# A tuned two-layer image kernel: softmax bookkeeping moved between engines, the last tile of a Winograd-type convolution summed in another order, and one tiny product moved

## The chip, the cores and the metric

The kernel runs on one core of one Trainium2 chip. The metric is the device time of that core in microseconds (us), the median of three runs. All data are 32-bit floats (f32). In what follows TensorE is PE, VectorE is DVE, ScalarE is ACT, GpSimd is POOL and SyncE, which only issues transfers here, is SP.

## The reference, cut to what matters

The input is `x` of shape (4, 256, 48, 48): four images, 256 channels, 2304 pixels each. Layer 0 is what the change touches:

```
h   = relu(batchnorm(conv3x3(groupnorm(x))))            # 256 -> 256 channels
q,k,v = qkv_w @ h + bias, 8 heads of 32 channels
attn = softmax(q^T k / sqrt(32))                          # 2304 x 2304 per head
x   = x + proj_w @ (v attn^T) + bias
```

Layer 1 normalizes the result, makes 45 softmax weights per pixel, applies five dilated 3x3 branches with them, mixes the six parts with a 1x1 convolution, normalizes over the batch and adds its input. It is not touched, but for images 1 to 3 its products share PE with the next image's convolution.

## The kernel before, in words

Per image b the kernel runs the 3x3 convolution, then q, k and v (`conv_qkv`), then the attention (`attention`), then layer 1 (`dynamic_filters`). The convolution and q, k, v of images 1 to 3 are fed into the layer 1 of the image before: a planner (`Clock`, `either`, `busy_dve`, the `need` and `free` entries) holds estimated times for each engine while the program is built, and by these it sets the order of PE's instructions and which engine does an elementwise step. The order is fixed when the program is built; on the chip every engine runs its own list in order, and semaphores tie the lists together.

**Attention.** An image's work is nine *units*. Units 0 to 7 are four heads (one half of the channels) by 512 queries; unit 8 is the last 256 queries of both halves. A unit has 18 steps, one for each 128 keys. A step m of unit u has these parts:

- `scores`: four products for four heads, one into the one-bank PSUM tile `so` (one buffer), three into the three-bank tile `se` (two buffers, shared with the denominators `den` and the projection `pp`).
- two exponentials on ACT, `p[:,0]` from `so` (L1350) and `p[:,1:]` from `se` (L1351).
- `weigh`: the numerator products of the step before, summed over the 18 steps in the PSUM tile `num` (one buffer, so the next unit's first product waits until `num` has been copied to `ao`), and the running sum `acc` of the exponentials on DVE (L1390). Five steps of a unit, the entries of `LENT` (two in unit 0, four in unit 8), *lend* three heads of their sum to a transfer from POOL's queue that adds `p[:,1:]` into a part of the tile `ring` called `extra` (L1392, L1394).

At the end of a unit ACT copies `num` (L1400) and DVE adds `extra` to `acc` (L1397). `close(u)` runs at step 1 of unit u+2: PE sums `acc` over the keys into `den` (L1406), and DVE transposes, inverts, transposes and multiplies (L1418 to L1428). `close(7)` runs at step 2 of unit 8. In unit 8 a product with a zero tile first clears the four heads' `num` (L1372), because its two halves write different columns. The order of the program in a step is: scores of this step, a `close` if due, `weigh` of the step before.

**Convolution of images 1 to 3** (`conv_blocks`). Along rows and along columns it uses sums of inputs and outputs, so that a tile (i, o) is four products n = 0 to 3 in two rotating PSUM buffers (`psc`). Product 0 is copied as `one`; products 0 and 1 give `two` (sum and difference); products 2 and 3 are joined with `two` to `y`; `after` adds the row term (`d12`, made in `before`) and asks for the relu (L1126) that writes `hid`. The last tile of the twelve is (5, 1), and the first q product (L1256) needs its relu.

**q, k, v.** Nine pairs of v products take turns in the same two PSUM buffers and are copied by ACT (L1285). `pb` (L1294) is a product of two columns that gives the bound of the scores, copied by DVE (L1295); it stands behind the last v.

**`ring`** also holds the convolution's weights: `taken(t)` has SP load 1024 columns for tile t; tile 0's are columns 2048 to 3071, loaded ahead of the attention.

Of the kernel before, what the change touches and what calls it, by code (L numbers as in the profile page):

```python
# [17 lines left out]
P = 128  # L18
# [40 lines left out]
def conv_preact_kernel(  # L59
# [493 lines left out]
    with tc.tile_pool(name="w", bufs=1) as wpool, tc.tile_pool(  # L553
# [554 lines left out]
        def conv_blocks(b, psum_tile, blocks, pool, hid):  # L1108
# [23 lines left out]
            def before(i, o):  # L1132

                s12, d12, s34, d34 = (blocks.held[:, j, o] for j in range(4))
                if i == 0:
                    t = spare.pop(0)
                    axpy(t, s34, -4.0, s12)
                    relu(o, 2, t, clock.both(800))
                    either(s12, s12, s34, ALU.subtract)
                elif i == 5:  # L1140
                    t = spare.pop(0)
                    axpy(t, d34, -2.0, d12)
                    relu(o, 1, t, clock.both(800))
                    axpy(d12, d34, -8.0, d12)
                    clock.both(800)

            def target(i, o):

# [3 lines left out]
                    return blocks.held[:, 1 if i == 2 else 3, o]  # L1152
                return spare.pop(0)

            def after(i, o, y):

                s12, d12, s34, d34 = (blocks.held[:, j, o] for j in range(4))
                if i in (2, 4):
                    s, d = (s12, d12) if i == 2 else (s34, d34)
                    either(s, y, blocks.first[o], ALU.add)  # L1160
                    either(d, blocks.first[o], y, ALU.subtract)
                elif i in (0, 5):
                    relu(o, i and 3, y, either(y, y, s12 if i == 0 else d12, ALU.add))

            blocks.scaled()
            need[0] = lambda: 150 + max(slot("c", 2), blocks.end[STEPS[0]])
            for t, (i, o) in enumerate(TILES):
                u = us.pop(t)
                y = target(i, o).rearrange("p (n s) -> p n s", s=2)
                for n, j in enumerate((1, 2, 0, 3)):  # L1170
                    m = psum_tile(f"pc_{b}_{i}_{o}_{j}")[:, :XN]
                    clock("PE", 0, slot("c", 2), blocks.end[i, j])
                    z = blocks.of[i].rearrange("p (j h n) -> p j h n", j=4, h=NH)[:, j]
                    relus(max(clock.t["ACT"], clock.t["PE"]))
                    for h in range(NH):
                        nc.tensor.matmul(
                            m, u[:, h, j], z[:, h], start=(h == 0), stop=(h == NH - 1)
                        )
                        clock("PE", MM * XN / CH)
                        if h == 0:  # L1180
                            need[0] = lambda: 0.0
                            if t == 1 and n == 3:
                                blocks.along(ORDER[1])
                            if n == 0:
                                if t + 2 < len(TILES):
                                    us[t + 2] = taken(t + 2)
                                before(i, o)
                            yield MM * XN / CH
                    if n == 0:
                        one = pool.tile([P, XN], F32, tag="one", name=f"one_{b}_{i}_{o}")  # L1190
                        nc.scalar.copy(one, m)
                        end = clock("ACT", 400, clock.t["PE"])
                    elif n == 1:
                        two = pool.tile([P, 2, XN], F32, tag="two", name=f"two_{b}_{i}_{o}")
                        if busy_dve():
                            nc.scalar.copy(two[:, 1], m)
                            end = clock("ACT", 400, clock.t["PE"])
                            either(two[:, 0], one, two[:, 1], ALU.add, end)
                            either(two[:, 1], one, two[:, 1], ALU.subtract, end)
                        else:  # L1200
                            tt(two[:, 0], m, one, ALU.add)
                            tt(two[:, 1], one, m, ALU.subtract)
                            end = clock("DVE", 900, clock.t["PE"], end)
                    else:
                        to = y[:, :, n - 2]
                        if busy_dve():
                            nc.scalar.mul(to, m, 1.0 if j == 0 else -1.0)
                            end = clock("ACT", 450, clock.t["PE"])
                            either(to, to, two[:, n - 2], ALU.add, end)
                        else:  # L1210
                            if j == 0:
                                tt(to, m, two[:, 0], ALU.add)
                            else:
                                tt(to, two[:, 1], m, ALU.subtract)
                            end = clock("DVE", 480, clock.t["PE"])
                        if n == 3:
                            after(i, o, y.rearrange("p n s -> p (n s)"))
                    free["c"].append(end)
                    then = STEPS[4 * t + n + 1] if 4 * t + n + 1 < len(STEPS) else None
                    need[0] = lambda: 150 + max(  # L1220
                        slot("c", 2), blocks.end.get(then, NEVER) if then else last[0],
                    )
                    if n == 3 and o == NH - 1:
                        blocks.passed.add(i)
                    if then is None:
                        relus(NEVER)
                        last[0] = clock.t["ACT"]
                    yield MM * XN / CH
# [4 lines left out]
        def conv_qkv(b, gn, psum_tile, weights, ready, pool, between=()):  # L1233
# [40 lines left out]
            for t in range(0, NT, 2):  # L1274
# [15 lines left out]
                    nc.vector.tensor_tensor(top[:, 0], top[:, 0], top[:, 1], ALU.mult)  # L1290
                    nc.vector.tensor_scalar(top[:, 0], top[:, 0], QS, None, ALU.mult)
                yield 4 * MM * C / CH
            pb = psum_tile(f"pb_{b}")
            nc.tensor.matmul(pb[:, :NH], hmat, top[:, 0], start=True, stop=True)  # L1294
            nc.vector.tensor_copy(bound[:, b, :], pb[:, :NH])  # L1295

        qkv = {}
        CONV_QKV = MM * (6 * 4 * 6 * TN / CH + NCK * NH * 4 + NT * 2 * C / CH)
# [6 lines left out]
        def attention(b, q, k_, vT, pools, spare, project, scratch, following):  # L1305
# [1 line left out]

            ps_s, ps_a, work0 = pools
            ao = keep("h", f"ao_{b}")
            zeros = work0.tile([P, D], F32, tag="zeros", name=f"zeros_{b}", bufs=1)  # L1310
            nc.gpsimd.memset(zeros, 0.0)

            extra = scratch.rearrange("p (j n) -> p j n", j=3)
            scratch = work0.tile([P, QC], F32, tag="rt", name=f"rt_{b}", bufs=1)

            whole, rest = N // QC * QC, N % QC
# [39 lines left out]
            def weigh(u, m, p):  # L1356
# [3 lines left out]
                        acc=work0.tile([P, 4, QC], F32, tag="acc", name=f"acc_{b}_{u}"),  # L1360
                    )
                st = state[u]
                several, end = len(units[u]) > 1, u == last
                if end and m >= NT - 2:
                    sums(u, p, m == NT - 2, m == NT - 1)
                    if m == NT - 2:
                        sums(u, st["acc"], False, False)
                        sums(u, extra, False, False, 1)
                if several and m == 0:

                    for j, r in enumerate(heads):
                        nc.tensor.matmul(st["num"][r, :], zeros, p[:, j, :], start=True, stop=False)  # L1372
                for i, (g, q0, n, at) in enumerate(units[u]):
                    for j, r in enumerate(heads):
                        nc.tensor.matmul(  # L1375
                            st["num"][r, at : at + n],
                            vT[:, m, g * P + j * D : g * P + (j + 1) * D],
                            p[:, j, at : at + n],
                            start=(m == 0 and not several),
                            stop=(m == NT - 1 and i == len(units[u]) - 1),  # L1380
                        )
                if end and m >= NT - 2:
                    return
                if m == 0:
                    st["first"] = p
                else:
# [2 lines left out]
                    js = slice(0, 1 if lend else 4)  # L1389
                    nc.vector.tensor_tensor(st["acc"][:, js], other[:, js], p[:, js], ALU.add)  # L1390
                    if lend and m == lends(u)[0]:
                        nc.gpsimd.dma_start(out=extra, in_=p[:, 1:])  # L1392
                    elif lend:
                        nc.gpsimd.dma_start(out=extra, in_=p[:, 1:], accum_op=ALU.add)  # L1394
                if m == NT - 1 and not end:
                    rest = st["acc"][:, 1:]
                    nc.vector.tensor_tensor(rest, rest, extra, ALU.add)  # L1397
                if m == NT - 1 and not end:
                    g, q0, n, _ = units[u][0]
                    nc.scalar.copy(ao[:, g, q0 : q0 + n], st["num"])  # L1400

            def sums(u, rhs, start, stop, first=0):
                if start:
                    state[u]["den"] = three(f"den_{b}_{u}")[:, 0, :]
                for j, r in enumerate(heads[first:]):
                    nc.tensor.matmul(  # L1406
                        state[u]["den"][r, :], ones, rhs[:, j, :], start=start, stop=stop
                    )

            def close(u):  # L1410

                if u < last:
                    sums(u, state[u]["acc"], True, True)
                else:
                    busy(ps_a.tile([P, 512], F32, tag="one", name="warm"), 5)
                st = state.pop(u)
# [15 lines left out]
            for i, (u, m) in enumerate(steps):  # L1432
# [5 lines left out]
                if prev is not None:  # L1438
                    weigh(*steps[i - 1], prev)
                prev = ps  # L1440
                if m == 2 and u == last:
                    close(u - 1)
                if m == 6 and (u % NH == 1 or u == last):
                    while (chunk + 1) * CH <= units[u if u == last else u - 1][0][1]:
# [935 lines left out]
        for b in range(B + 1):  # L2380
# [176 lines left out]
            if b == B - 1:  # L2557
# [1 line left out]
                    out=pads[B % 2].rearrange("p h r w -> p (h r w)")[:, : NH * (2 + NF) * CH],  # L2559
                    in_=late_d[0].rearrange("p m c -> p (m c)"),  # L2560
                )
            scratch = ring[:, : 3 * QC]
            spare = []
            following = [lambda: None] * 2
            clear(pads[b % 2] if b else pads[1])
            if b + 1 < B:
                load_pad(b + 1)
                us[0] = taken(0)

                def opened(b=b):  # L2570
                    coming.append(Blocks(b + 1, pads[(b + 1) % 2]))
                    coming[-1].stage0()
                    us[1] = taken(1)
# [97 lines left out]
```

## Time and profile before

| what | us |
|---|---|
| median of three runs | 2675.72 |
| lowest and highest of them | 2675.06, 2680.87 |
| the profiled execution, its own time | 2675.02 |
| its span, first to last instruction | 2673.2 |
| PE busy | 2586.6 (97%) |
| DVE busy | 2080.8 (78%) |
| ACT busy | 1802.6 (67%) |
| POOL busy | 789.6 (30%) |

Busy times are counted from the records of the instructions, and a matmul's end is modelled, so that a busy PE may be one that waits; only starts are to be relied on. A row of the timeline has the start, the length, the engine (PEld are PE's weight loads), the line, the operation, the output and inputs, the shape and the count; in square brackets the idle time of the engine before it and what ended that. The four attentions begin at 151, 798, 1446 and 2069 us.

### The profile page before, as it was taken

To read this page: it belongs to the slowest core of one execution; us is meant where nothing else is said; L and a number is where in the kernel's file an instruction comes from. 1 tells how busy PE (TensorE), PEld (TensorE's weight loads), DVE (VectorE), ACT (ScalarE), POOL (GpSimd) and SP (SyncE) were. 2 spreads that over 40 slices of the span, in tenths; PEclk is the share of its full clock that TensorE was granted. 3 is DMA by queue.
4 is the path that set the end of the run, shared out by engine and by line. 5 is a ranking of instruction groups with operands and counts; after the bars stand their busy time and mean duration, and the time that the engine had idled before them with its cause. 6 is when DMAs were issued, how large, how long until landed. Compare 5 with 4: busy or idle time off the path is not lost. (4 is left out here: it accounts for less than half of the span.)

```text
span 2673.2 us, 42578 instructions
## 1 busy us (share of the span) xinstructions
PE 2586.6 (97%) x16952; PEld 1092.1 (41%) x16952; DVE 2080.8 (78%) x2045; ACT 1802.6 (67%) x2281; POOL 789.6 (30%) x885
## 2 busy tenths in 40 slices
PE   7999999999999999999999999999989999999996
PEld 5632222555562222355555222245546222235554
DVE  7768998858739898967764989895775889895676
ACT  4479898734449999854445998984444989884344
POOL 4201001286520011057750001007765000100453
PEclk9999999999999999999999999999999999999998
DMA  4815445323252445433324354452324544433456
GB/s 174 225 42 107 101 101 114 92 65 103 70 108 72 101 95 114 102 81 89 95 63 91 89 113 101 101 108 79 89 69 125 128 106 95 107 84 79 121 165 222
DMA packets 138094, 279.96 MB, mean 105 GB/s; under 512 B 58152, under 2 KB 98512, under 8 KB 136864
## 3 DMA queue, kind: packets, MB, share of 16 engines
q0 software_dynamic: 27408, 144.00, 23.1%
q1 hardware_dynamic: 110480, 133.17, 18.9%
q8 instruction: 135, 2.21, 0.3%
q14 instruction: 71, 0.58, 0.1%
HBM read 112.12 MB, written 36.04 MB: 55 GB/s over the span
## 5 line engine op out<-in xcount | busy, mean ns | idle before, releaser
L1390 DVE TENSOR_TENSOR acc<-acc,p 128x2048 f32<-128x2048 f32 (+1 forms) x568 | 1039.3, 1830 | 96.7 <-ACT p L1351 46.2
L1351 ACT ACTIVATE p<-se 128x1536 f32<-128x1536 f32 x648 | 938.7, 1449 | 0.0
L1340 PE MATMUL se<-q,k 32*128 32x512 f32 (+1 forms) x4320 | 737.0, 593 | 0.0
L1340 PE MATMUL so<-q,k 32*128 32x512 f32 (+1 forms) x1440 | 728.3, 593 | 3.5 <-DVE bound L1295 2.0
L1375 PE MATMUL num<-p,vT 128*32 128x512 f32 (+1 forms) x5760 | 699.4, 561 | 1.7 <-ACT ao L1400 1.7
L1350 ACT ACTIVATE p<-so 128x512 f32<-128x512 f32 x648 | 388.5, 600 | 158.7 <-PE se L1340 63.1
L1340 PEld LDWEIGHTS so<-q,k 32*128 32x128 f32 x1440 | 216.5, 183 | 517.8 <-ACT p L1350 477.0
L1843 POOL TENSOR_TENSOR near<-near,prod 128x384 f32<-128x384 f32 x352 | 352.6, 1034 | 225.9 <-DVE prod L1837 222.8
L1394 POOL DMA_DIRECT2D ring<-p x128 | 109.1, 852 | 796.2 <-ACT p L1351 615.7
L1375 PEld LDWEIGHTS num<-p,vT 128*32 128x32 f32 x5760 | 129.0, 108 | 475.4 <-issue 448.9
L1837 DVE TENSOR_TENSOR prod<-wb,pad 128x768 f32<-128x768 f32 x192 | 182.1, 954 | 86.4 <-ACT wb L1824 53.1
L1340 PEld LDWEIGHTS se<-q,k 32*128 32x128 f32 x4320 | 227.1, 183 | 5.1 <-ACT p L1351 4.3
L1824 ACT COPY wb<-ws 128x384 f32<-128x384 f32 x216 | 108.7, 507 | 171.9 <-DVE prod L1837 127.9
L1392 POOL DMA_DIRECT2D ring<-p x36 | 20.1, 558 | 574.5 <-DVE ao L1428 274.1
L2001 PE MATMUL py<-far,wsc 128*128 128x384 f32 x512 | 169.9, 487 | 0.0
L1545 PE MATMUL pg<-pad,wcat 128*45 128x384 f32 x864 | 146.7, 490 | 8.8 <-ACT lg L1603 8.8
L1256 PE MATMUL pq<-hid,wqkv 128*128 128x384 f32 x384 | 133.9, 503 | 15.0 <-ACT hid L1126 12.8
L1513 ACT COPY far<-far 128x512 f32<-128x512 f32 x86 | 90.3, 1108 | 79.8 <-PE far L1771 76.4
L2001 PEld LDWEIGHTS py<-far,wsc 128*128 128x128 f32 x512 | 96.2, 190 | 66.0 <-issue 1.8
L1256 PEld LDWEIGHTS pq<-hid,wqkv 128*128 128x128 f32 x384 | 73.5, 195 | 69.6 <-ACT hid L1126 15.1
L1390 DVE TENSOR_TENSOR acc<-p,p 128x2048 f32<-128x2048 f32 x36 | 82.3, 2285 | 21.3 <-ACT p L1351 14.8
L1745 DVE COPY_PREDICATED amat<-along_y,bmat 128x768 f32<-128x768 uint32 x72 | 93.1, 1293 | 2.4
(336 smaller groups left out, 2836.7 us busy)
## 6 DMA issues: line engine op xcount, KB each, us to landing
ring<-p POOLq DMA_DIRECT2D x164, 768.0 KB, 5.7
ws<-w_d SPq DMA_DIRECT2D x216, 192.0 KB
ring<-u_d SPq DMA_DIRECT2D x36, 512.0 KB
pad<-in_x SPq DMA_DIRECT2D x14, 1152.0 KB
xst<-in_x POOLq DMA_DIRECT2D x36, 192.0 KB, 3.6
x_d<-pad SPq DMA_DIRECT2D x36, 192.0 KB
u_d<-pad SPq DMA_DIRECT2D x12, 512.0 KB
y_d<-y SPq DMA_DIRECT2D x13, 384.0 KB
```

The lines of the kernel that those rows point to most:

```text
L1256: nc.tensor.matmul(pq[:, :CH], wqkv[:, i, s, g * P : (g + 1) * P], hid[:, i, cols], start=(i == 0), stop=(i == NH - 1),)
L1340: nc.tensor.matmul(dst[:, at : at + n], k_[r, g, m * P : (m + 1) * P], q[r, g, q0 : q0 + n], start=True, stop=True,)
L1350: nc.scalar.activation(p[:, 0, :], s1, AF.Exp, scale=QS)
L1351: nc.scalar.activation(p[:, 1:, :], s3, AF.Exp, scale=QS)
L1375: nc.tensor.matmul(st["num"][r, at : at + n], vT[:, m, g * P + j * D : g * P + (j + 1) * D], p[:, j, at : at + n], start=(m == 0 and not s ...
L1390: nc.vector.tensor_tensor(st["acc"][:, js], other[:, js], p[:, js], ALU.add)
L1394: nc.gpsimd.dma_start(out=extra, in_=p[:, 1:], accum_op=ALU.add)
L1545: nc.tensor.matmul(pg[64 * s : 64 * s + NG, :CH], wcat[:, ii, k, :], shifted(ii, cc, k // 3 - 1, k % 3 - 1), start=(i == 0 and k == 0), st ...
L1824: nc.scalar.copy(pw[:, :CH], fetched[c, k][0])
L1837: nc.vector.tensor_tensor(prod.rearrange("p h (r w) -> p h r w", w=WW), wb, src, ALU.mult)
L1843: nc.gpsimd.tensor_tensor(cat[:, h], cat[:, h], prod[:, h], ALU.add)
L2001: nc.tensor.matmul(py[c][:, o, :CH], wsc[:, n * NH + i, o * P : (o + 1) * P], rhs, start=(n == 0 and i == 0), stop=(n == order[-1] and i = ...
```

## The change

Four things are altered.

1. The last tile of the convolution, (5, 1), takes its row term ahead: `base` is the term and its due time, `two` is made of `one` plus the two interleaved halves of the term as soon as product 0 is there, product 1 is added and subtracted, and products 2 and 3 then give `y` complete, always by DVE from PSUM.
2. `pb` and its copy stand behind the fifth pair of v products (t = 8), with an entry in the planner.
3. The unit's `extra` is one of two parts of `ring` (six times 512 columns, even and odd units). For units 0 to 6 a POOL transfer adds `acc[:,1:]` into `extra` in place of DVE's add, and `den` reads `acc[:,0]` and `extra`. Unit 7 keeps DVE's add. Tile 0's weights are loaded in `opened`, after the attention's last step. `close(7)` runs at step 3, after `weigh`.
4. `num` is copied to `ao` by DVE, ahead of the unit's last `acc` add. The zero tile and its product are gone; in unit 8 the first half's product starts the sum, and the second half's does not.

In PE's list of 16952 matmul records nothing else is moved; the planner leaves every other step in its place, except that in image 3 the last tile's `two` and `y` go from POOL to DVE and POOL in turn.

```diff
@@ before(i, o) in conv_blocks
-                    either(s12, s12, s34, ALU.subtract)
-                elif i == 5:
+                    return s12, either(s12, s12, s34, ALU.subtract)
+                if i == 5:
...
-                    clock.both(800)
+                    return d12, clock.both(800)
@@ after(i, o, y, end)
-                    relu(o, i and 3, y, either(y, y, s12 if i == 0 else d12, ALU.add))
+                    if not TILES.index((i, o)) + 1 == len(TILES):
+                        end = either(y, y, s12 if i == 0 else d12, ALU.add)
+                    relu(o, i and 3, y, end)
@@ the loop over products
-                                before(i, o)
+                                base = before(i, o)
...
-                    if n == 0:
+                    if n == 0 and base and t + 1 == len(TILES):
+                        one = pool.tile([P, XN], F32, tag="one", name=f"one_{b}_{i}_{o}")
+                        nc.scalar.copy(one, m)
+                        end = clock("ACT", 400, clock.t["PE"])
+                        two = pool.tile([P, 2, XN], F32, tag="two", name=f"two_{b}_{i}_{o}")
+                        for s in range(2):
+                            tt(two[:, s], one, base[0][:, s::2], ALU.add)
+                        base = clock.both(960, base[1], end)
+                    elif n == 1 and base and t + 1 == len(TILES):
+                        if busy_dve():
+                            one = pool.tile([P, XN], F32, tag="one", name=f"uno_{b}_{i}_{o}")
+                            nc.scalar.copy(one, m)
+                            end = clock("ACT", 400, clock.t["PE"])
+                            either(two[:, 0], two[:, 0], one, ALU.add, end)
+                            either(two[:, 1], two[:, 1], one, ALU.subtract, end)
+                        else:
+                            tt(two[:, 0], m, two[:, 0], ALU.add)
+                            tt(two[:, 1], two[:, 1], m, ALU.subtract)
+                            end = clock("DVE", 900, clock.t["PE"], base)
+                    elif n == 0:
...
-                        if busy_dve():
+                        if busy_dve() and t + 1 < len(TILES):
@@ conv_qkv
-            pb = psum_tile(f"pb_{b}")
-            nc.tensor.matmul(pb[:, :NH], hmat, top[:, 0], start=True, stop=True)
-            nc.vector.tensor_copy(bound[:, b, :], pb[:, :NH])
+                if t == 8:
+                    pb = psum_tile(f"pb_{b}")
+                    nc.tensor.matmul(pb[:, :NH], hmat, top[:, 0], start=True, stop=True)
+                    nc.vector.tensor_copy(bound[:, b, :], pb[:, :NH])
+                    free["c"].append(clock("DVE", 200, clock("PE", 100, slot("c", 2))))
@@ attention
-            extra = scratch.rearrange("p (j n) -> p j n", j=3)
+            extra = scratch.rearrange("p (s j n) -> p s j n", s=2, j=3)
...
-                if several and m == 0:
-                    for j, r in enumerate(heads):
-                        nc.tensor.matmul(st["num"][r, :], zeros, p[:, j, :], start=True, stop=False)
...
-                            start=(m == 0 and not several),
+                            start=(m == 0 and i == 0),
...
+                if m == NT - 1:
+                    g, q0, n, _ = units[u][0]
+                    nc.vector.tensor_copy(ao[:, g, q0 : q0 + n], st["num"])
...
                 if m == NT - 1 and not end:
                     rest = st["acc"][:, 1:]
-                    nc.vector.tensor_tensor(rest, rest, extra, ALU.add)
-                if m == NT - 1 and not end:
-                    g, q0, n, _ = units[u][0]
-                    nc.scalar.copy(ao[:, g, q0 : q0 + n], st["num"])
+                    if u == last - 1:
+                        nc.vector.tensor_tensor(rest, rest, extra[:, u % 2], ALU.add)
+                    else:
+                        nc.gpsimd.dma_start(out=extra[:, u % 2], in_=rest, accum_op=ALU.add)
+                        rest = extra[:, u % 2]
+                    st["parts"] = [st["acc"][:, 0], *(rest[:, j] for j in range(3))]
...
-                if m == 2 and u == last:
+                if m == 3 and u == last:
                     close(u - 1)
@@ the loop over images
-            scratch = ring[:, : 3 * QC]
+            scratch = ring[:, : 6 * QC]
...
-                us[0] = taken(0)
 
                 def opened(b=b):
+                    us[0] = taken(0)
                     coming.append(Blocks(b + 1, pads[(b + 1) % 2]))
```

## The prediction

> **What bounds the kernel now.** The page first: its busy row names PE.
>
> ```profile
> PE 2586.6 (97%) x16952; PEld 1092.1 (41%) x16952; DVE 2080.8 (78%) x2045; ACT 1802.6 (67%) x2281; POOL 789.6 (30%) x885
> ```
>
> A modelled end hides short waits inside "busy", so I went on to the timeline and took PE's starts of each `scores`. A plain step of the attention takes 2.07 us. The excess stands at the unit boundaries, the same in all four images: +0.49 at unit 1 (step 1: 2.56); +0.86 and +0.46 at units 2 to 7 (steps 1 and 2: 2.93, 2.53), of which 0.88 is the `den` product; +1.73, +0.86 and +0.22 at unit 8. Here is the boundary of unit 2, image 0:
>
> ```profile
> 228.04 2.29 DVE L1390 TENSOR_TENSOR acc<-acc,p 128x2048 f32<-128x2048 f32 x1
> 228.40 0.69 PE L1340 MATMUL so<-q,k 32*128 32x512 f32 x1
> ...
> 229.31 0.59 ACT L1400 COPY ao<-num 128x512 f32<-128x512 f32 x1
> ...
> 229.48 1.07 PE L1406 MATMUL den<-acc,ones 128*32 128x512 f32 x8
> 229.78 0.63 ACT L1350 ACTIVATE p<-so 128x512 f32<-128x512 f32 x1
> ...
> 230.26 1.49 ACT L1351 ACTIVATE p<-se 128x1536 f32<-128x1536 f32 x1
> 230.36 1.04 PE L1375 MATMUL num<-p,vT 128*32 128x512 f32 x8
> ...
> 231.33 0.69 PE L1340 MATMUL so<-q,k 32*128 32x512 f32 x1
> 231.80 0.30 PEld L1340 LDWEIGHTS se<-q,k 32*128 32x128 f32 x6 [0.18 <-ACT p L1351]
> ```
>
> Read: the copy (229.31) pushes the two exponentials; the second ends at 231.75, and only then can the next `se` start (231.80), 0.47 after its `so`.
>
> Outside the attention I asked PE's waits alone, then the two places that the change touches: the wait for `hid` (image 1), and `pb` (image 0).
>
> ```profile
> PE pq L1256 <- ACT hid L1126: 12.8, 4, 6.1
> ```
>
> ```profile
> 726.94 1.62 DVE L1105 TENSOR_TENSOR cv_q<-cv_q,two 128x288 f32<-128x288 f32 x2
> ...
> 728.59 1.43 DVE L1105 TENSOR_TENSOR cv_q<-cv_q,cv_v 128x576 f32<-128x576 f32 x1
> ...
> 730.06 0.87 ACT L1126 ACTIVATE hid<-cv_q,bn_t_f,bn_s 128x576 f32<-128x576 f32 x1 [3.44 <-DVE cv_q L1105]
> ...
> 730.98 0.59 PE L1256 MATMUL pq<-hid,wqkv 128*128 128x384 f32 x1 [2.95 <-ACT hid L1126]
> ```
>
> ```profile
> 149.84 0.28 PE L1294 MATMUL pb<-qktop,hmat 128*128 128x2 f32 x2
> ...
> 150.15 0.16 DVE L1295 COPY bound<-pb 128x2 f32<-128x2 f32 x1 [13.85 <-PE pb L1294]
> ...
> 150.37 1.05 PE L2482 MATMUL pb<-vbc,wp 128*128 128x1 f32 x8 [0.25 <-DVE bound L1295]
> ```
>
> **The copy on DVE, units 2 to 7.** 32 ACT copies of 0.59 become 32 DVE copies. The trace has no such copy; its nearest row is the transpose out of PSUM of the same shape, 0.71 (L1418), and DVE's add of that shape takes 0.69. I take 0.69. The copy waits for the last `num` product (227.40 plus about 1.0) and for the add ahead of it (ends 227.94): 228.41 to 229.10. Behind it in DVE's list the last `acc` add goes from 228.04 to 229.2, ending 231.5, and the transpose comes at 231.6, ahead of today's 232.04, since L1397's 1.76 is gone. PE's `num` product stands behind `den`, at 230.36, so a copy ready by 229.15 gains nothing there. ACT gains: the exponential of `so` starts when its scores are out, 229.56 (1.16 after their start, as in plain steps), `se`'s ends 1.95 later at 231.51, and PE's `se` starts at 231.56 in place of 231.80. That is 0.24, six times per image: 24 x 0.24 = 5.8 us saved. What is late next is the same release, by 0.23.
>
> **Unit 1.** No `den` covers `num` here, and DVE is late: the add of step 16 ends at 191.35 (unit 0 lends twice only), so the copy runs 191.45 to 192.14 and `num` starts at 192.19, today 192.22. The other images give +0.01, +0.01, -0.13. The visible 0.49 stays: 0.1 us saved in all; bounds 0 and 4 x 0.49 = 2.0.
>
> **Unit 8, no zero product.** PE loses 0.86 (472.72 to 473.58). Followed on: `num` at 472.72, scores 2 at 473.69 (its `se` at 473.92), scores 3 at 475.97. But unit 7 keeps L1397, and copy and wait put the DVE list back: last add 471.6, L1397 at 473.9, transpose of `den` 6 at 475.6 to 476.3, and the `se` of scores 3 needs that buffer. Scores 4 come at 479.3 (today 479.78), but then `den` 7's transpose stands behind two adds, ends at 481.9, and holds the `se` of scores 5; the `num` product after it starts at 483.0, today 482.9. So 0; bounds 4 x 0.86 = 3.4 saved and 0.8 lost.
>
> **The merge.** 28 DVE adds of 1.76 leave a list that isn't PE's bound: 0. In their place POOL issues 28 transfers; one waits on POOL's queue for the last `acc` add (231.5), and behind it stands the next unit's first lending, whose `p` comes at 234.45. `den` reads the result over 30 us later; an adding transfer of this size lands in 5.7. Here a rule speaks against the change. L1390's 2048-wide adds, beside 164 such issues:
>
> ```profile
> L1390 DVE TENSOR_TENSOR acc<-acc,p x568: 684/2292/2295, 158.7 to 2429.7; 128x2048 f32<-128x2048 f32 x138, 128x512 f32<-128x512 f32 x52
> ```
>
> The longest is 2.295, 3 ns over the median. The Trainium skill (GPSIMD Engine Reference, Specifications) says that GpSimd's way into SBUF is shared with VectorE and contended by DVE instructions with two SBUF inputs, as these adds are. By the rule an add beside each of 28 more issues (0.85 each) might stretch by up to that, 24 us of DVE, of which a unit has some 2 us to spare (38.3 less 12 x 2.39 + 5 x 0.79 + 0.79 + 0.5 + 2.39 = 36.3), so still 0 on PE; by the row nothing stretches. I take the row.
>
> **Tile 0's weights.** The load goes behind ten `x_d` stores on SP, the last issued by 491; `ring` is free there since unit 7. The first product is at 521.86: 0. If it waited for the attention's end (514.2), some 6 us remain.
>
> **The last tile.** In images 1 and 2 three DVE steps fall away between product and relu: two of 288 (1.62) and one of 576 (1.43). DVE now joins products 2 and 3 from PSUM, 0.45 each (nearest rows L1212, L1214: at most 0.46, POOL busy or not, while L1105's two-SBUF add runs 0.44 to 1.26). Behind `prod` (to 727.0): joins 726.94 to 727.76, relu 727.80 to 728.67, q at 728.72 in place of 730.98: 2.26 saved; image 2 alike. The q products before the wait move from 727.11 to 727.44 (their buffer is now freed by DVE) and still end ahead. The new early steps are covered: DVE's two adds of the term follow it at 708.3, POOL's two for product 1 are done by about 711 (one of them is there today), and products 2 and 3 come at 724.4; if that cover were gone, they would cost their 2.5. ACT is spared two copies of 0.41, POOL the zero tile's 0.12, neither on PE's path. Image 3 waits longest (6.10, to 1993.99) and gains least: POOL does most there today, beside DVE's term. Without POOL's adds beside them DVE's predicated copy and two term steps shrink (1.46, 1.33, 1.25 to about 1.02, 0.75, 0.75), the term is ready at 1989.5, two adds to 1990.45, POOL's two (0.8 each) to 1991.75, joins to 1992.25, relu to 1993.15: q at 1993.2, 0.8 saved; bounds 1 lost, 2 saved. Sum 5.3 us saved.
>
> **`pb` amid v.** Today it costs image 0 0.53 (149.84 to 150.37). In images 1 and 2 the first scores wait for the last v's copy anyway, and in image 3 for statistics that read the bank (L1874 ends 2068.78; the wait is put down to `bound`, 0.06 later). Among the v's, PE runs without gaps. In images 0 to 2 the next v gets `pb`'s buffer and waits for the copy: 0.53 each. In image 3 it gets the fifth v's, just ended, and waits for ACT's copy: 0.1 to 0.2 latency, 0.59, 0.05, so 0.83. A second rule: Perfetto Trace Analysis, Optimizing Tensor Performance, has groups rotate through PSUM banks so that a copy runs beside the next group. By it `pb` costs only its 0.21; by the row, where one buffer pair serves both, 0.53 to 0.83. Image 0: 0; 1 and 2: +0.53; 3: +0.83 - 0.1. Sum 1.8 us lost (by the rule, 0.2: 0.21 in each image, less the 0.53 and the 0.1). I take the row.
>
> **Sum.** -5.8 - 0.1 + 0 - 5.3 + 1.8 = -9.4. The profiled execution took 2675.02, 0.7 under the median, both within the runs' spread; off the median, 2666.3 us.
>
> **Rivals.**
> - More is won (2660): unit 8 keeps its 0.86 and unit 1 half of its 0.49, -3.4 and -1.0, and image 3 gains 2 more. For: all are PE time today. Against: the DVE times above. 0.15.
> - The convolution's gain is given back, because the pairs after it are held by ACT and DVE (their rows show 36.9 and 24.8 us of ACT waiting for PE, so they are not): -5.8 + 1.8, 2671.7, within 0.2%. 0.15.
> - DVE becomes the attention's bound: more issues on POOL stretch the adds. It decides from 2 us per unit; six issues stretching 0.5 each make 3, so 1.0 lost in 28 units: 2694. Against: the 2.295. 0.04.
>
> That the order differs from what the diff says is excluded: the built lists show it.
>
> **The numbers.** A measurement here tells about 0.2%, 5.35 us, from no change. Main case 0.66, with its bounds (unit 8, unit 1, image 3, `pb`) 2662 to 2670. Faster is main and first rival, 0.81; same 0.15; slower 0.04. The range reaches to both nearer rivals: 2660.5 to 2672.
>
> **What would show it.** Steps 1 and 2 of units 2 to 7 at 2.93 and 2.29; unit 1's step 1 still over 2.45; unit 8's steps 1 to 5 sum to 13.2 as today, with `se` waiting for L1418's successor; q's waits 0.4, 0.4 and about 5.3; a gap of 0.5 to 0.8 behind `pb`. Wrong if acc adds run over 2.3, if unit 1 falls to 2.1, or if a v waits for nothing.

## The result and the profile after

| | median us | runs | before, beside it | ratio and its 95% interval |
|---|---|---|---|---|
| changed kernel | 2666.04 | 6 (2658.96 to 2669.89) | 2678.03 | 0.9955 (0.9943 to 0.9967) |

The changed kernel is 12 us faster, by the interval 9 to 15; predicted were 9.4 and 2666.3. The profiled execution of it spans 2665.3 us, 7.9 less than that of before. Its busy row, its row of the 2048-wide adds and the landing time of the new transfers:

```profile
PE 2582.2 (97%) x16920; PEld 1093.8 (41%) x16920; DVE 2046.0 (77%) x2053; ACT 1787.6 (67%) x2243; POOL 805.7 (30%) x908
...
ring<-acc POOLq DMA_DIRECT2D x28, 768.0 KB, 5.7
```

```profile
L1412 DVE TENSOR_TENSOR acc<-acc,p x568: 691/2291/2295, 160.1 to 2421.3; 128x2048 f32<-128x2048 f32 x138, 128x512 f32<-128x512 f32 x52
```

The longest add is 2.295 us as before. Of the 28 new issues, though, only 4 run beside such an add (2.282 to 2.284); the other 24 run beside the transposes and the reciprocal of `den`, which have one input and keep their lengths too (0.71, 0.25, 0.71). That an issue stretches no add is shown by the lendings, of which 164 ran beside an add before and 160 after. The boundary of unit 2 in image 0 (timeline; PE's rows stand some 1.1 us later than before, the last add 2.24 later, since the copy is now ahead of it):

```profile
229.67 0.69 DVE L1405 COPY ao<-num 128x512 f32<-128x512 f32 x1 [0.60 <-PE num L1394]
...
230.28 2.28 DVE L1412 TENSOR_TENSOR acc<-acc,p 128x2048 f32<-128x2048 f32 x1
...
230.61 0.62 PE L1432 MATMUL den<-acc,ones 128*32 128x512 f32 x1
...
231.18 1.45 ACT L1374 ACTIVATE p<-se 128x1536 f32<-128x1536 f32 x1
...
232.47 0.69 PE L1363 MATMUL so<-q,k 32*128 32x512 f32 x1
232.47 0.71 DVE L1445 STREAM_TRANSPOSE rt<-den 128x512 f32<-128x512 f32 x1
...
232.68 0.71 PE L1363 MATMUL se<-q,k 32*128 32x512 f32 x3
```

The copy takes the 0.69 that was taken for it. The exponential of `se` ends at 232.63, and `se` follows its `so` by 0.21, before by 0.47. At the boundary of unit 1 in image 0 the copy stands right behind the add of step 16, the second of the first row's two:

```profile
188.01 4.69 DVE L1412 TENSOR_TENSOR acc<-acc,p 128x2048 f32<-128x2048 f32 x2
...
192.62 0.68 DVE L1405 COPY ao<-num 128x512 f32<-128x512 f32 x1
...
193.36 1.06 PE L1394 MATMUL num<-p,vT 128*32 128x512 f32 x8 [0.19 <-DVE ao L1405]
```

The two places outside the attention, image 1:

```profile
728.69 0.45 DVE L1233 TENSOR_TENSOR cv_q<-pc,two 128x288 f32<-128x288 f32 x1
...
729.05 0.44 DVE L1235 TENSOR_TENSOR cv_q<-two,pc 128x288 f32<-128x288 f32 x1
...
729.53 0.87 ACT L1126 ACTIVATE hid<-cv_q,bn_t_f,bn_s 128x576 f32<-128x576 f32 x1 [1.82 <-DVE cv_q L1235]
...
730.45 0.91 PE L1279 MATMUL pq<-hid,wqkv 128*128 128x384 f32 x2 [0.35 <-ACT hid L1126]
...
788.98 0.28 PE L1318 MATMUL pb<-qktop,hmat 128*128 128x2 f32 x2
...
789.30 0.16 DVE L1319 COPY bound<-pb 128x2 f32<-128x2 f32 x1 [6.97 <-PE pb L1318]
789.51 7.17 PE L1301 MATMUL pv<-wqkv,hid 128*128 128x256 f32 x32 [0.25 <-DVE bound L1319]
```

The wait of 2.95 for `hid` is now 0.35 (and 0.26 for the first product), and `pb` holds the next v by 0.53. Two of PE's waits stand out now: one for `wq`, which no part of the change was meant to touch (2.5 us in all before), and that of image 3's join (longest 5.4, before 6.1).

```profile
PE wT L1750 <- DMA wq<-w_d: 5.9, 6, 2.3
...
PE pq L1279 <- DVE cv_q L1233: 5.9, 3, 5.4
```

Starts of PE's instructions cut the execution into stages. "Join" runs from the twelfth-last record of the convolution's products to the first v, "v" from there to the first scores, "attention" to its last products, "rest" is what lies between (image 0's own join, 39.93 in both, is left out). The last column is the kernel before with fillers in PE's waits (run e9 below).

| stage, image | before | after | predicted | measured | e9 |
|---|---|---|---|---|---|
| join, 1 | 76.62 | 72.87 | -2.26 | -3.75 | 75.14 |
| join, 2 | 77.89 | 72.88 | -2.27 | -5.01 | 75.15 |
| join, 3 | 48.53 | 47.39 | -0.8 | -1.14 | 46.68 |
| v, 0 to 3 | 17.91, 15.75, 15.75, 37.30 | 17.91, 16.27, 16.27, 38.16 | +1.8 | +1.90 | as before, image 3 37.58 |
| attention, 0 to 2 | 365.34, 365.21, 365.39 | 363.30, 363.34, 363.34 | -4.4 | -5.96 | as before |
| attention, 3 | 367.58 | 363.03 | -1.5 | -4.55 | 365.00 |
| rest, 0 to 3 and the end | 93.51, 189.04, 188.87, 171.89, 225.27 | 94.86, 191.46, 189.49, 177.61, 225.60 | 0 | +10.4 | 93.44, 188.50, 189.63, 171.94, 225.27 |

So the total was right, but it is the sum of more gains than I saw and of losses that I didn't see. The runs separate most of them.

### The profile page after: what moved, and what is told of

Its sections match the earlier page's. It is cut to its first block, busy times and chain, and to the rows that moved or that the text cites. A ratio compares the mean times of both kernels' runs of the same rounds, so it can differ in the third digit from the quotient of the medians.

```text
span 2665.3 us, 42523 instructions
## 1 busy us (share of the span) xinstructions
PE 2582.2 (97%) x16920; PEld 1093.8 (41%) x16920; DVE 2046.0 (77%) x2053; ACT 1787.6 (67%) x2243; POOL 805.7 (30%) x908
## 5 line engine op out<-in xcount | busy, mean ns | idle before, releaser
L1424 POOL DMA_DIRECT2D ring<-acc x28 | 23.9, 853 | 243.7 <-DVE acc L1412 243.7
```

## The experiments

All were timed in five rounds beside the kernel before.

| run | median us | before | ratio and interval |
|---|---|---|---|
| e1, copy alone | 2699.86 | 2680.59 | 1.0070 (1.0058 to 1.0082) |
| e2, copy back on ACT | 2671.89 | 2680.59 | 0.9970 (0.9959 to 0.9981) |
| e3, zero product back | 2663.02 | 2680.59 | 0.9939 (0.9926 to 0.9952) |
| e4, `pb` behind v | 2666.34 | 2680.59 | 0.9941 (0.9928 to 0.9955) |
| e5, old last tile | 2674.68 | 2677.61 | 0.9987 (0.9979 to 0.9994) |
| e6, before with fillers | 2677.77 | 2677.61 | 1.0001 (0.9993 to 1.0009) |
| e7, three lendings in unit 0 | 2664.67 | 2677.61 | 0.9948 (0.9935 to 0.9961) |
| e8, den amid scores | 2693.53 | 2677.61 | 1.0050 (1.0037 to 1.0064) |
| e9, fillers sized | 2666.03 | 2676.09 | 0.9960 (0.9947 to 0.9974) |
| e10, ends and `pb` | 2661.99 | 2676.09 | 0.9944 (0.9931 to 0.9958) |
| e11, the same, one more filler set | 2664.55 | 2677.19 | 0.9953 (0.9940 to 0.9967) |

An interval is 4 to 7 us wide, so effects of 1 or 2 us are read from the traces: PE's time from the first score product of a step to that of the next, image 1.

```
unit 2, steps 0 to 5            unit 8, steps 1 to 6
before 2.07 2.94 2.53 2.07 2.07 2.07    3.80 2.93 2.29 2.08 2.08 4.91
after  2.07 2.94 2.27 2.07 2.07 2.07    2.94 2.28 3.20 2.08 2.45 4.85
e1     2.07 2.94 2.27 2.35 2.59 2.33    3.79 2.94 2.29 3.13 2.08 4.92
e2     2.07 2.93 2.53 2.07 2.07 2.07    2.94 2.54 2.93 2.29 2.08 4.91
e3     2.07 2.94 2.27 2.07 2.08 2.07    3.80 2.08 2.94 2.29 2.08 4.91
e8     2.07 2.07 4.11 2.07 2.07 2.07    2.08 4.12 2.93 2.29 2.08 4.91
```

**e1: the copy without the merge.**

```diff
@@ before, weigh
+                if m == NT - 1:
+                    g, q0, n, _ = units[u][0]
+                    nc.vector.tensor_copy(ao[:, g, q0 : q0 + n], st["num"])
                 if m == 0:
...
-                if m == NT - 1 and not end:
-                    g, q0, n, _ = units[u][0]
-                    nc.scalar.copy(ao[:, g, q0 : q0 + n], st["num"])
```

> The kernel before with one edit: num is copied to ao by VectorE, ahead of the unit's last acc add, and no longer by ScalarE; VectorE keeps its 32 ring adds and the zero product stays. Theory (ScalarE's copy held the exponentials, VectorE has room): steps 1 and 2 of units 2 to 7 go from 2.93, 2.53 to 2.93, 2.29 as in the changed kernel, 24 x 0.24 = 5.8 us; unit 1's step 1 goes from 2.56 to about 2.36 (0.8 us over four images); unit 8 keeps 13.2 for steps 1 to 5. Median some 6.5 us below before (ratio 0.9975). Rival (the merge made the room): with the ring add of 1.76 still in VectorE's list the transpose of den ends 0.7 us later than before, holds the se of the third scores, and what step 2 gains step 3 loses: steps 1 to 3 of units 2 to 7 still sum to 7.53; less than 1.5 us in all.

19 us slower by the timed runs and 24 in the profiled execution, worse than either theory. Step 2 wins its 0.26, but steps 3 to 5 lose 0.28, 0.52 and 0.26: 0.80 net in each of 24 units, and 1.05 in unit 8. The timeline of e1 at the boundary of unit 2, image 0:

```profile
228.66 2.28 DVE L1393 TENSOR_TENSOR acc<-acc,p 128x2048 f32<-128x2048 f32 x1
...
230.97 1.76 DVE L1400 TENSOR_TENSOR acc<-acc,ring 128x1536 f32<-128x1536 f32 x1
...
232.65 0.71 DVE L1418 STREAM_TRANSPOSE rt<-den 128x512 f32<-128x512 f32 x1
...
233.41 0.71 PE L1340 MATMUL se<-q,k 32*128 32x512 f32 x3
...
237.41 0.60 ACT L1350 ACTIVATE p<-so 128x512 f32<-128x512 f32 x1 [1.19 <-DVE acc L1393]
```

With the ring add of 1.76 still in the list, the transpose ends at 233.36 and `se` of scores 3 waits for that buffer (233.41, 0.29 after its `so`); then DVE's adds come late and two steps on an exponential waits 1.19 for the `p` that an add still reads. The rival, which said that the merge made the room, is right, and understated it.

**e2: the merge without the copy.**

```diff
@@ after, weigh
-                if m == NT - 1:
-                    g, q0, n, _ = units[u][0]
-                    nc.vector.tensor_copy(ao[:, g, q0 : q0 + n], st["num"])
...
                     st["parts"] = [st["acc"][:, 0], *(rest[:, j] for j in range(3))]
+                if m == NT - 1 and not end:
+                    g, q0, n, _ = units[u][0]
+                    nc.scalar.copy(ao[:, g, q0 : q0 + n], st["num"])
```

> The changed kernel with the num copy back on ScalarE, behind the unit's last acc add; the merge by transfer and all else stay. Theory: steps 1 and 2 of units 2 to 7 go back to 2.93 and 2.53 and unit 1's step 1 to 2.56; 6.6 us lost against the changed kernel (span near 2672). Rival (the ring add taken off VectorE also released something): step 2 stays under 2.45, and less than 3 us are lost.

Steps 1 and 2 are 2.93 and 2.53 again, unit 1's step 1 2.55, and the median is 5.9 above the changed kernel's. Alone the merge is worth 0 in units 2 to 7, as predicted, and the copy alone costs 19; together they win 6. In unit 8 steps 1 to 5 are 0.17 shorter with the copy on ACT, and step 6 is 0.06 longer.

**e3: the zero product back.** Edit: the tile, its memset and the four products of before, and `start=(m == 0 and not several)`.

> The changed kernel with the zero tile's product back in unit 8 (four heads, 0.86 us of TensorE at step 1). Theory of the prediction (unit 8 is bound by VectorE's list there): steps 1 to 5 sum to about what they do without it, 13.0 to 13.2, the product's time falling into a wait of the next steps for the se buffer. Rival (the product is on the path): step 1 is 3.80 and the sum 13.8, 0.86 more in each image, 3.4 us in all. Everything outside unit 8 unchanged.

Step 1 is 3.80 again, but step 2 falls to 2.08: steps 1 to 5 sum to 13.19, without the product to 12.95. Of the product's 0.86 about 0.24 is on the path. The median, 3 us below the changed kernel's, can't show this; outside unit 8 the trace differs most in the rest of image 3, 172.00 against 177.61 (below).

**e4: `pb` behind v.**

```diff
@@ after, conv_qkv
-                if t == 8:
-                    pb = psum_tile(f"pb_{b}")
...
+            pb = psum_tile(f"pb_{b}")
+            nc.tensor.matmul(pb[:, :NH], hmat, top[:, 0], start=True, stop=True)
+            nc.vector.tensor_copy(bound[:, b, :], pb[:, :NH])
```

> The changed kernel with pb and its copy back behind the last v. Theory of the prediction (pb amid v stalls the next v for its buffer, and behind v its wait is hidden by the last v's copy): images 1 to 3 gain 0.5 to 0.8 each between the first v and the first scores, image 0 nothing: 1.8 us faster. Rival (the scores' start waits for something else, whichever place pb has): from the first v to the first scores of every image within 0.2 us of the changed kernel. A third way: image 0 loses 0.53 by it and the others gain nothing, 0.5 slower.

First v to first scores: 17.91, 15.75, 15.75, 37.26, so 0, 0.52, 0.52 and 0.90 less: the prediction's step, image by image. Unit 0's step 1, which is 2.54 in images 1 and 2 of the changed kernel, is 2.43 as before. The attention of image 3, though, took 365.55 in place of 363.03, and the medians are equal. That difference led to the next runs.

**e5: the old last tile.** Edit: the two `base` branches switched off, `after` adds the term again.

> The changed kernel with the convolution's last tile formed as in the kernel before (row term added at the end, in after). Theory of the prediction: the wait for hid comes back, 2.26 us in images 1 and 2 each and 0.8 in image 3, 5.3 us in all. Rival (a wait of TensorE costs twice: itself, and a half-clock stretch of 3.41 us in the clock records that follows it): images 1 and 2 lose about 4.1 each from the first q product to the first v, 2.26 by the wait and up to 1.7 by the clock, some 9 us in all with image 3.

8.6 us slower than the changed kernel; join 76.64 and 76.64 in images 1 and 2, 3.77 more each: near the rival's 4.1 and far from the theory's 2.26. The clock records have a stretch of 3.41 us at half clock behind each of the two waits (from 733.9 and 1382.4).

**e6 and e9: the kernel before, its waits filled.**

```diff
@@ before, conv_qkv
                         pq = psum_tile(f"pq_{b}_{c}_{g}_{s}")
+                        if b and not (c or g or s):
+                            for _ in range(8 if b == B - 1 else 4):
+                                nc.tensor.matmul(
+                                    pq[:, :CH], wqkv[:, 0, 0, :P], hid[:, 0, cols],
+                                    start=True, stop=True,
+                                )
...
             pb = psum_tile(f"pb_{b}")
+            if b == B - 1:
+                for _ in range(2):
+                    nc.tensor.matmul(
+                        pb[:, :CH], wqkv[:, 0, 0, :P], hid[:, 0, :CH], start=True, stop=True
+                    )
```

That is e9; e6 had 14 and 8 in the first place and 4 in the second.

> The kernel before with filler products (128x384, their results overwritten) that keep TensorE busy in its waits and shorten none: eight ahead of the first q product of images 1 and 2, fourteen in image 3, and four ahead of pb in image 3. Theory (TensorE's clock is halved for one or two stretches of 3.41 us after a wait of 2 to 6 us): no half-clock stretch at these four places, the products behind the waits run at full pace; images 1, 2 and 3 gain 1.3 to 3.4 each between the first q product and the first scores, the first scores of image 3 gain 2.2; 6 to 9 us faster than before, near 2671, with no other change. Rival (what stands behind the waits isn't bound by TensorE, or the stretches come all the same): within 1 us of before.

e6 was a miss in size: a filler is two records and took 0.65 us, so in image 1 eight took 5.3, and `hid` was there 3.9 after the first of them began. The half-clock stretches at the four places were gone, but the overshoot ate the gain.

> The kernel before with fillers again, now sized by what one took in the run before this (0.65 us each, two records): four ahead of the first q product of images 1 and 2, eight in image 3, two ahead of pb in image 3, so that each set ends before its wait does. Theory (a wait of TensorE is followed by a half-clock stretch that costs up to 1.7 us more): from the first q product to the first v 1.3 us less in images 1 and 2 each (55.24 to about 54.0), the attention of image 3 from 367.6 to 365.3; some 5 us faster than before (near 2673) at a mean clock of 0.994 to 0.995. Rival (the filled time, not the clock, decides): within 1 us of before.

10 us faster than before, twice what was expected and as much as the whole change brought, with nothing made shorter; in the profiled execution it is 8.2, by the table 6.1 in the joins and 2.6 in image 3's attention, less 0.3 for the fillers ahead of it. Rows of the windows view (window; its length; busy us of PE, PEld, DVE, ACT, POOL with counts; granted clock; DMA share; GB/s), first before, then e9, each for the stretch behind image 1's wait and for the one that begins 0.6 after image 3's first scores:

```profile
731.50:734.90 3.40, 3.40 (x11) 1.68 (x10) 2.06 (x3) 1.98 (x4) 1.44 (x2) 0.50 0.28 57
2069.50:2076.30 6.80, 6.16 (x32) 1.24 (x24) 1.01 (x1) 3.88 (x4) 0.00 (x0) 0.50 1.01 188
```

```profile
730.90:734.30 3.40, 3.40 (x16) 2.08 (x15) 2.40 (x3) 2.67 (x5) 1.46 (x2) 1.00 0.22 56
2063.80:2070.60 6.80, 6.11 (x52) 1.42 (x45) 2.29 (x1) 5.71 (x6) 0.00 (x0) 1.00 1.01 192
```

In the same 3.40 us PE issues 16 matmul records in place of 11; in the 6.80 of image 3 52 (48 where the stretch is laid 0.2 later) in place of 32. So a wait of PE costs itself and, behind it, up to half of 3.41 or 6.83 us. The join falls from 76.62 to 75.14 by the clock alone; from there to the changed kernel's 72.87 it is 2.27, and 2.27 in image 2, for 2.26 and 2.27 predicted. In image 3, where e11 has no half-clock stretch either, the change itself is 46.68 to 45.83, 0.85 for 0.8.

**e7: unit 0 lends three times.** The kernel that ran had only the last of the three edits named here, `FIRST = (6, 10, 14)`; the two on unit 7 came with e10.

> The changed kernel with three edits at the ends of the attention: unit 7 too is merged by a POOL transfer and close(7) comes at step 6 of unit 8, with the projection at step 9; unit 0 lends at steps 6, 10 and 14 in place of 9 and 14. Theory (VectorE's list is what is late there): unit 1's step 1 goes from 2.33 to 2.38 down to about 2.1, 0.27 in each image; steps 1 to 9 of unit 8 from 24.05 to about 23.6; some 3 us in all. Rival: the landing of unit 7's transfer or the third lending is late, den or an exponential waits for it, and nothing or less is gained.

Unit 1's step 1 is 2.07 in every image (after: 2.33 to 2.38), as a plain step, and the attention is 0.2 shorter. DVE being late was all of that step's excess.

**e8: `den` between `so` and `se`.**

> The changed kernel with the den products of units 2 to 8 between the so and the se products of step 2 in place of step 1's end, so that they lie in the wait of se for its buffer. Theory (the 0.21 left of step 2 is se waiting for the exponential): step 1 falls to 2.07 and step 2 rises to 2.95, 0.2 saved in each of 28 units, 5.6 us. Rival (num of that step then waits for an exponential that starts 0.88 later, or num of step 1 for VectorE's copy without den's cover): steps 1 to 3 sum to 7.28 as now, nothing is gained.

Steps 1 to 3 sum to 8.25 in place of 7.28, 27 us in all. Neither theory: the timeline of e8 shows what both left out.

```profile
230.36 1.12 PE L1369 MATMUL so<-q,k 32*128 32x512 f32 x2
...
232.41 1.13 PE L1369 MATMUL se<-q,k 32*128 32x512 f32 x6
...
233.60 1.45 ACT L1380 ACTIVATE p<-se 128x1536 f32<-128x1536 f32 x1 [1.48 <-PE se L1369]
```

In the other kernels `so` and `se` start together and take 1.07 us in all: the four heads' products, of 32 rows each (32*128 in the rows), run side by side. Parted, each takes its 1.05, and ACT waits 1.48 for the exponential of `se`.

**e10 and e11: towards a faster one.** The changed kernel with unit 0's three lendings, unit 7 merged by transfer like the others, `close(7)` at step 6 and the projection at step 9, `pb` behind v with two fillers in image 3.

> The changed kernel with what the runs so far point to: unit 0 lends at steps 6, 10 and 14; unit 7 is merged by a POOL transfer as well, close(7) at step 6 of unit 8 and the projection at step 9; pb back behind v, with two fillers ahead of it in image 3. Theory: unit 1's step 1 at 2.07 (0.2 us an image), steps 1 to 9 of unit 8 from 24.05 to about 23.6 (0.5 an image), v to scores 0.5, 0.5 and 0.9 less in images 1 to 3, no half-clock stretch at the first scores of image 3: 4.5 us below the changed kernel, near 2661.5. Rival (the late den of unit 7 pushes its division past the projection, which then waits): unit 8 gains nothing or loses, and 2663 to 2665 is left.

All steps came: unit 1's step 1 2.07; steps 1 to 9 of unit 8 23.61 (after: 24.04); v to scores 15.75, 15.75 and 37.22; no half clock at image 3's scores. The median is 4 us under the changed kernel's, as expected, but the intervals overlap. e11 adds eight fillers ahead of the first q product of image 3.

> The kernel of the run before this (changed kernel, three lendings in unit 0, unit 7 merged by transfer, pb behind v with two fillers in image 3), and eight more fillers in image 3's wait ahead of the first q product, into a PSUM bank that is free there. Theory: the wait of 5.4 us stays, the half-clock stretch behind it goes; first q product to first v in image 3 from 38.1 to 38.9 down to about 37.3, and the median about 1.5 us lower, near 2660.5. Rival (what follows that wait is held by ScalarE's and VectorE's joins and not by TensorE): within 0.5 us of the run before.

That stretch is gone (join 45.83, e10 46.61), but five others stand in the filters' stages, four in e10, and the median is 2.6 higher. By the timed runs the two, and the changed kernel, are not told apart.

## Why the prediction was right, point by point

- **Copy, units 2 to 7: right.** Steps 2.93 and 2.29 predicted, 2.93 and 2.28 measured; 24 x 0.255 = 6.1 for 5.8.
- **Merge at 0: right as a number, wrong as a reason.** "A list that isn't PE's bound" holds only while the copy is on ACT. e1 shows that the merge carries the copy.
- **Unit 1: the step that failed is the copy's start.** I let it begin 0.1 after the add of step 16 ended. It began 0.08 before the end of that add's record (192.62 against 192.70, rows above), `num` started 3.40 after the unit's first scores in place of 3.59, and step 1 fell to 2.33 to 2.38, not "over 2.45". 0.8 won in place of 0.1.
- **Unit 8: mis-sized.** Scores 2 and 3 came when the chain said (5.02 and 7.30 after the unit's start, predicted 5.01 and 7.29), with `se` behind the transpose. Scores 4 came 0.12 earlier than forecast, and the transpose of `den` 7, which holds the `se` of scores 5 as forecast, ended 12.91 after the unit's start and not 13.22. 0.23 an image and 0.06 in step 6, 1.2 in all, in place of 0. By e2 0.4 an image would have been won there with the copy on ACT (steps 1 to 9 in 23.92, before 24.32, after 24.04).
- **Last tile: the wait right, the sum not.** -5.3 predicted, -5.4 with the clock held equal, -9.9 in the trace. The missing term is the half-clock stretch behind the wait: 1.5 in image 1, 2.7 in image 2, where the stretch lasted 6.83. Before's trace had it, in the granted clock, and I never asked for it there.
- **`pb`: right, and the row beat the rule.** 0, 0.52, 0.52, 0.86 measured for 0, 0.53, 0.53, 0.73; the 0.21 that I took from the rotating-banks rule does not hold where one pair of buffers serves both.
- **Adds beside POOL's issues:** no stretch, the row was right. But I set an add beside each of the 28 new issues, and only 4 had one; those 4 alone would prove little.
- **Left out: +10.4 in "rest".** 1.35 of it is in the first stage, which scatters from 91.95 to 95.32 over all kernels. 5.7 are in image 3, where a cause can be named (next section but one). The other 3.4 aren't settled. In images 1 and 2 the changed kernel's clock records have a half-clock stretch of 3.41 each (from 559.2 and 1286.3), and before's have none; but e9, the kernel before with fillers, has the second too (from 1287.3), with 0.76 more in that stage. The load of tile 0's weights, which I put at 0, now falls beside the first `wq` loads, but it wasn't moved alone.

So the total came out in part by luck. With the clock held equal the four changes won 11.6 (6.1 + 0.8 + 1.2 + 5.4 - 1.9) for the 9.4 forecast; the clock added some 7 (4.5 in the joins, 2.6 in image 3's attention, which is chance, see below), and "rest" took 10.4, which leaves about 8 in the profiled execution. Over the six runs the gain is larger, 12.

## What to carry to other kernels

Ask for the granted clock behind every wait of PE near 2 us or more: where a half-clock stretch follows, removing the wait is worth both, and a few products that fill a wait bring the second part without the first. Price edits that share an engine's list together, for one can be worth nothing alone and still be what lets the other pay. Where an experiment is to tell a few tenths, read starts in the trace, not medians.

## What the runs showed of the hardware

- **The clock works on a grid.** In each of 13 profiles all half-clock stretches between 100 us and the tail start at whole multiples of 3.413 us from one another. Laying that grid over PE's records (150 us to 40 us before the end): all 30 windows with no PE record for 1.95 us or more in sum were followed by half clock, 7 of 20 windows with 1.6 to 1.95. The rule is one-sided: 26 of the 63 half-clock windows came behind shorter idle times, 11 of these as the second of a pair, so idle time isn't the whole condition. By it a wait of 2.0 to 2.2 us is sure to count only if it falls into one window. With `pb` behind v and no fillers image 3's first scores were hit in 3 profiles of 3, with `pb` amid v in 1 of 6 (e8). The wait is 2.0 us in the three and 2.1 in the six, so by this grid that is chance rather than `pb`'s doing, and I don't count those 2.6 us (367.58 to e9's 365.00) to the change. The Trainium skill (TensorE: Matmul & The Clock Gate, Part 1) has the free-running window of 3413 ns, which agrees; its advice to avoid idle gaps over about 3.4 us is too generous here.
- **An instruction fetch seems to delay a transfer.** The SP queue holds the fifteenth set of `wq` loads until a store has landed, 2.2 us of wait before and 3.8 after:

```profile
SPq L1635 <- DMA w_d<-lg: 2.2, 1, 2.2
```

```profile
SPq L1662 <- DMA w_d<-lg: 3.8, 1, 3.8
```

In the changed kernel the instruction queue has one packet of 16 KiB in that window:

```profile
q8 instruction: 1, 0.02, 0.5%
```

It starts 4.2 us after the store was issued. In the 8 profiles with a packet there, `wq` is issued 6.2 to 6.4 after the store; in the 5 without (the four on the kernel before, and e3) 4.7 to 4.8. PE then waits for `wq` 2.1 to 2.4 us in the 8 and 0.5 to 0.9 in the 5, and in 6 of the 8 (not e2 and e5) a half-clock stretch begins at that wait or within 2 us of it; image 3's "rest" is 175.2 to 177.6 in the 8, 171.9 to 172.7 in the 5. In the changed kernel the longer wait (1.7) and half of its stretch of 6.83 make, by estimate, 5.1 of the 5.7. e3 differs from the changed kernel only by the zero tile and its products and has no packet there, so an edit elsewhere can move it. The Trainium skill (Runtime: NRT & Kernel Launch, Instruction fetch mechanics) calls the cost of going from one 16 KiB block to the next mostly hidden; here one such fetch goes with a delay of 1.5 us. That the packet causes the delay is inferred from 13 of 13 agreeing, e3 among them, and not shown by moving it alone.
